# A hand-written order for the last two pairs of a two-layer graph kernel, and the norms at the change of passes in two parts

## The chip, the cores and the metric

The kernel runs on one core of a Trainium2 chip. The metric is the device time of one execution in microseconds (us), as the median of three runs. The engines are named as the profile names them: PE is TensorE (PEld its weight loads), DVE is VectorE, ACT is ScalarE, POOL is GpSimd, SP is the engine that only issues DMAs here. Each engine runs its own list of instructions strictly in order and waits on semaphores.

## The reference

Two graph layers on `x` of 128 graphs x 64 nodes x 768 features, with an adjacency of ones and zeros. Both are of the form `x + layer(relu(layernorm(x)))`.

```python
# layer 0: three products of 768 x 768 after neighbour averages, plus a table of relations
ctx = matmul(adj, hs @ Wadj.T + badj) / deg + matmul(radj, hs @ Wrev.T + brev) / rdeg + hs @ Wself.T + bself
rel = einsum('bij,bijr->bir', adj, E[rels]) @ Wr.T + br * deg + ...      # and the same for the reverse
# layer 1: attention with 6 heads of 128, and a gate
h = einsum('bni,hio->bhno', feat_in, W);  th = tanh(h)
attn = leaky(th @ w_src + (th @ w_dst).T);  attn = softmax(where(adj == 0, -999, attn))
feat_out = elu(concat(attn @ h + b))
gate = sigmoid(feat_in @ H_w.T + H_b)
out = gate * feat_out + (1 - gate) * feat_in
```

The result of layer 1 is added to its input `x`.

## The kernel before

The 8192 rows (graphs x nodes) are cut into 64 tiles of 128 rows (two graphs each), and these into 32 pairs. The kernel makes two passes over the pairs, one for each layer. Everything is float32.

**Products.** In both passes the products of a pair with the 768 x 768 weights go through a fast scheme for a 2 x 3 by 3 x 3 block product: 15 block products instead of 18. `A_SUMS` are the 11 sums f1 to f11 of the activations' blocks (`a00` to `a12`: first digit the tile of the pair, second the third of the features), `B_SUMS` those of the weights' blocks, `PRODUCTS` the 15 products, each with its PSUM bank (a, b, c or d), the output block it adds to and the sign. In pass 2 a product computes the heads' block (columns of `W`) and the gate's block (columns of `H_w`) side by side: `half_product` (L742) issues one matmul of 512 columns, 256 for the heads and 256 for the gate, and two of them make a product. `read` (L763) and `read_act` (L759) add the bank to the result in `hzs`: most reads are one DVE instruction of 512 columns over both halves; where a block gets its first value, ACT copies the heads' half and DVE adds the bias to the gate's half (256 columns each). A bank can be written again only when it has been read.

**Pass 1** is left to a scheduler. Its `finish` (L582) normalizes a pair's result for layer 1. For each tile k: `stats` (L229) takes mean and deviation on DVE (L233, L237, L239), the power -1/2 on POOL (L240) and the scaled mean on DVE (L241); ACT makes `hf` = relu of the norm (L588), which SP stores; POOL adds it to x (L590), SP stores that to the output; ACT makes `hh`, half of hf plus a half (L593), which SP stores. `hf` and `hh` share two buffers, so each waits until the one two before it has been stored.

**Pass 2** has its engines' order written out by hand: `ORDER` lists the steps of one pair, each with a lag (`R8/1` is the read of product 8 of the pair before), and the loop at its end walks this list for every pair; only SP is ordered by the scheduler. Steps: `Ta00` transposes a block on PE, `Ca00` copies it to SBUF on ACT (L732), `Ff1` forms a sum on DVE (L256, L258), `P1.0` is the first half of product 1, `R1` and `RA1` its reads on DVE and ACT. Then for each tile (0 or 1 of the pair): `th` tanh (L783), `mul` the products with w_src and w_dst (L787), `sum` their row sums on ACT (L797), `k` and `chain` the splitting of the sums in bf16 parts on POOL (L800 to L810), `rows`, `rrow`, `lrow`, `log` the logits (L822 to L839), `memset`, `cp`, `pre`, `tr`, `exp`, `rec` the masked softmax (L835 to L864), `turnp`, `pT` its transpose, `swap` a copy of heads between partitions by DMA (L816), `att` the attention (L888), `ev` the division, with bias, into f (L898, in two groups: even and odd heads), `g` the gate (L905), `e` the exponential (L909), `f0` to `f2` the end on DVE (L916, L918, L920), and `dma` the store (L923): POOL issues a DMA that adds f to the x which pass 1 stored in the output. A tile's f has two buffers.

Pair 31's `finish`, the last, runs within the first round of pass 2, in one piece at a quarter of the list, since pass 1 has no round after it. The bias `bb` of the heads (plus one) is loaded at the start of pass 2 (L682) and gets its one on DVE at L685.

Of the kernel before, what the change touches and what calls it, by code (L numbers as in the profile page):

```python
# [8 lines left out]
F32 = mybir.dt.float32  # L9
BF16 = mybir.dt.bfloat16  # L10
I32 = mybir.dt.int32
AF = mybir.ActivationFunctionType
OP = mybir.AluOpType
AX = mybir.AxisListType

P = 128
# [64 lines left out]
ORDER = """  # L81
# [6 lines left out]
turnp1/2 RA2 Ff11 e0/2 P1.1 P8.0 mul1/1 RA1 R1 P5.1 g1/1 pT1/2 rows0/1 R3 P4.0 lrow0/1 P6.0  # L88
f0.0/2 g0/1 att1/2 sum1.2/1 rec1/2 rrow0/1 f0.1/2 sum1.0/1 sum1.3/1 RA5 ev1.1/2 log0/1 swap1/1
sum1.1/1 swap0/1 P6.1 R5 ev1.0/2 e1/2 P4.1 P8.1 k1/1 R4 cp0/1 pre0/1 memset1/1 R6 P11.0 f1.0/2  # L90
""".split()


@with_exitstack
def kernel(
# [45 lines left out]
    nc = tc.nc  # L141
    G, N, D = x.shape
# [5 lines left out]
    H, DO = w_src.shape  # L148
# [32 lines left out]
    def row(v, parts):  # L181

        n = 1
        for s in v.shape:
            n *= s
        return bass.AP(tensor=v.tensor, offset=v.offset, ap=[[0, parts], [1, n]])
# [33 lines left out]
    dl = const.tile([P, H], F32, name="dl")  # L220
    nc.gpsimd.memset(dl, 0.0)

    def row_constants():
        for c in range(3):
            for i in range(NPART):
                a = c * HB + i * H
                nc.sync.dma_start(dl[a : a + H, :], ident[0:H, 0:H])

    def stats(src, to, behind=False):  # L229

        st = small.tile([P, 2, 6], F32, name="st")
        for i in range(2):
            ins = nc.vector.bn_stats(st[:, i, :], src[:, i * HALF : (i + 1) * HALF])  # L233
            if behind and i == 0:
                tc.keep_in_program_order(ins)
        mv = small.tile([P, 2], F32, name="mv")
        nc.vector.bn_aggr(mv, st.rearrange("p a b -> p (a b)"))  # L237
        ve = small.tile([P, 1], F32, name="ve")
        nc.vector.tensor_scalar(ve, mv[:, 1:2], EPS, None, op0=OP.add)  # L239
        nc.gpsimd.tensor_tensor(to[:, 0:1], ve, mhalf, op=OP.pow)  # L240
        nc.vector.scalar_tensor_tensor(to[:, 1:2], mv[:, 0:1], -1.0, to[:, 0:1],  # L241
                                       op0=OP.mult, op1=OP.mult)

# [59 lines left out]
    with ExitStack() as px:  # L305
# [273 lines left out]
                steps.append(lambda b=b, c=c: (counts(b, c, True), add(b, c)))  # L579
            return steps  # L580

        def finish(p):  # L582
            for k in range(2):
                t = 2 * p + k
                to = small.tile([P, 2], F32, name="rn")
                stats(X[t], to)
                h = keep.tile([P, D], F32, name="hf", bufs=2)
                nc.scalar.activation(h, X[t], AF.Relu, scale=to[:, 0:1], bias=to[:, 1:2])  # L588
                nc.sync.dma_start(H1D[p][k * P : (k + 1) * P, :], h)
                nc.gpsimd.tensor_add(X[t], X[t], h)  # L590
                nc.sync.dma_start(of[t * P : (t + 1) * P, :], X[t])
                hh = keep.tile([P, D], F32, name="hh", tag="hf", bufs=2)
                nc.scalar.activation(hh, h, AF.Identity, scale=0.5, bias=half)  # L593
                nc.sync.dma_start(HHD[p][k * P : (k + 1) * P, :], hh)

        def side(p):

# [46 lines left out]
                (24, lambda: count(0, 1)), (26, lambda: digits(0)),  # L644
                (68, lambda: count_t(0, 0)), (68, lambda: count_t(0, 1))]
        for p in range(NP):
            more = [(3, lambda: finish(p - 1))] if p else late
            if p == 1:
                more.append((10, row_constants))
            if p == NP - 1:  # L650
                more += fetch()
            merged(main(p), own(p) + side(p + 1) + more)


    with ExitStack() as px:
# [20 lines left out]

        load(0)
        hzs += [wb.tile([P, 2, D], F32, name=f"hz{i}") for i in range(4, NHZ)]

        bb = wb.tile([P, DO], F32, name="bb")  # L680
        wsd = wb.tile([P, 2, D], F32, name="wsd")
        nc.sync.dma_start(bb, row(b_att, P))  # L682
        nc.sync.dma_start(wsd[:, 0, :], row(w_src, P))
        nc.sync.dma_start(wsd[:, 1, :], row(w_dst, P))
        nc.vector.tensor_scalar(bb, bb, 1.0, None, op0=OP.add)  # L685
        mone = wb.tile([P, 1], F32, name="mone")
        nc.gpsimd.memset(mone, -1.0)
        de = wb.tile([P, H, N], BF16, name="de")
# [245 lines left out]
        def step(n, p):  # L934
            if n[0] in "TCF":
                {"T": turn, "C": copy, "F": form}[n[0]](p, n[1:])
            elif n[0] == "P":
                half_product(p, *(int(i) for i in n[1:].split(".")))
            elif n[0] == "R":
                (read_act if n[1] == "A" else read)(p, int(n.lstrip("RA")))  # L940
            elif "." in n:
                m, i = n.split(".")
                OF_TILE_PART[m[:-1]](2 * p + int(m[-1]), int(i))
            else:
                OF_TILE[n[:-1]](2 * p + int(n[-1]))

        order = [(n, int(k or 0)) for n, _, k in (x.partition("/") for x in ORDER)]
        px.enter_context(tc.manual_schedule(engines={
            mybir.EngineType.PE, mybir.EngineType.DVE, mybir.EngineType.Activation,
            mybir.EngineType.Pool}))  # L950
        for i in range(min(k for _, k in order), NP + max(k for _, k in order)):
            if i >= 0:
                load(i + 1)
            for j, (n, k) in enumerate(order):
                if i == 0 and j == len(order) // 4:
                    finish(NP - 1)
                if 0 <= i - k < NP:
                    step(n, i - k)


# [43 lines left out]
```

## Time and profile before

| | |
|---|---|
| median of 3 runs | 2537.05 us (2536.32 to 2537.84) |
| the profiled execution's own time | 2537.99 us |
| its span, first to last instruction | 2536.2 us |
| PE busy | 2460.0 us, 97% |
| DVE busy | 1983.1 us, 78% |
| ACT busy | 1073.5 us, 42% |
| POOL busy | 438.3 us, 17% |
| first transpose of pass 2 | at 1515.1 us |
| one round of pass 2 | 30.2 us (from the reciprocal of one pair, L864 at 2412.33, to the next at 2442.55) |
| last product of pass 2 starts | at 2491.07 us |

The page's busy times and slices are of one execution. A timeline's line gives the start in us from the span's start, the duration, the engine, the line of the kernel and the operation, what it writes and reads, and in brackets how long the engine stood idle before it and what ended that. In a window's row the numbers are the window, its length, and the busy time of PE, PEld, DVE, ACT and POOL with counts, then the granted clock of PE (1.00 is full), the DMA engines' share and GB/s. Consecutive DVE instructions overlap by about 0.085 us in the records, so an instruction of 0.42 us takes 0.335 us of the engine.

### The profile page before, as it was taken

How to read it: one execution, taken by the hardware profiler on the slowest of the kernel's cores; microseconds unless marked ns; L12 is line 12 of the kernel's file. 1: busy time of each engine (PE TensorE's matmuls, PEld its weight loads, DVE VectorE, ACT ScalarE, POOL GpSimd, SP SyncE). 2: the span in 40 equal slices, each digit the busy share in tenths (PEclk: the TensorE clock that was granted, in tenths of full speed). 3: DMA queues.
4: the chain of work that ended last, by engine and by line, in shares of the span. 5: the costliest groups of instructions: out<-in, count | busy, mean ns of one | idle time of the engine just before them, and what ended most of it. 6: DMA issues, size and time to landing. Idle time of an engine off the chain costs nothing.

```text
span 2536.2 us, 35252 instructions
## 1 busy us (share of the span) xinstructions
PE 2460.0 (97%) x12012; PEld 1713.6 (68%) x12012; DVE 1983.1 (78%) x4115; ACT 1073.5 (42%) x3586; POOL 438.3 (17%) x799
## 2 busy tenths in 40 slices
PE   5999999999999999999999998999999999999994
PEld 4788888888888888888888883444444444444442
DVE  8987777777777777777777555888888888888886
ACT  1222221222222212222222214777777777777775
POOL 0112121121221211212112111111111111111111
PEclk8999999999999999999999999999999999999996
DMA  5112122121121211211212143444444444444433
GB/s 174 58 53 104 52 82 74 52 104 53 59 98 53 91 66 53 104 53 69 88 53 99 52 150 118 102 104 106 102 107 110 102 108 110 109 114 103 96 75 75
DMA packets 114758, 224.17 MB, mean 88 GB/s; under 512 B 36506, under 2 KB 48397, under 8 KB 114578
## 3 DMA queue, kind: packets, MB, share of 16 engines
q1 hardware_dynamic: 105208, 196.70, 23.7%
q0 software_dynamic: 9216, 25.17, 6.4%
q8 instruction: 94, 1.54, 0.2%
q14 instruction: 86, 0.70, 0.1%
q10 hardware_dynamic: 154, 0.06, 0.0%
HBM read 95.67 MB, written 100.66 MB: 77 GB/s over the span
## 4 chain that ended last, share of the span: by engine, by line
PE 93%; DVE 2%; DMA 2%; issue 2%; POOL 1%; ACT 0%; SPq 0%; POOLq 0%; DVEq 0%; ACTq 0%
PE pwa L560 19%; PE pwb L560 16%; PE pma L745 13%; PE pmb L745 11%; PE pwc L560 7%; PE pwd L560 6%; PE pb L513 5%; PE pmc L745 5%; PE pmd L745 4%; PE ps L888 2%; PE ps L721 2%; PE pwd L544 1%; PE ps L870 1%; PE ps L839 1%; DVE weights L258 0%
## 5 line engine op out<-in xcount | busy, mean ns | idle before, releaser
L560 PE MATMUL pwa<-weights,op 128*128 128x256 f32 x2304 | 543.2, 383 | 4.5 <-DVE x L552 3.8
L560 PEld LDWEIGHTS pwa<-weights,op 128*128 128x128 f32 x2304 | 423.7, 190 | 73.6 <-DVE x L552 12.5
L521 ACT COPY op<-pb 128x768 f32<-128x768 f32 x160 | 124.2, 798 | 756.3 <-PE pb L513 756.3
L560 PE MATMUL pwb<-weights,op 128*128 128x256 f32 x1536 | 372.4, 383 | 11.4 <-DVE x L554 7.8
L258 DVE TENSOR_TENSOR op<-op 128x768 f32<-128x768 f32 x256 | 238.9, 953 | 156.0 <-ACT op L521 156.0
L560 PEld LDWEIGHTS pwb<-weights,op 128*128 128x128 f32 x1536 | 285.8, 191 | 59.1 <-DVE x L554 8.6
L745 PE MATMUL pma<-weights,op_f 128*128 128x512 f32 x640 | 318.0, 594 | 1.2 <-DVE weights L774 1.2
L797 ACT ACTIVATE pr<-pr 128x128 f32<-128x128 f32 x768 | 225.2, 295 | 24.2 <-DVE pr L787 24.2
L745 PE MATMUL pmb<-weights,op_f 128*128 128x512 f32 x384 | 197.4, 596 | 0.0
L745 PEld LDWEIGHTS pma<-weights,op_f 128*128 128x128 f32 x640 | 115.9, 191 | 120.3 <-issue 108.6
L240 POOL TENSOR_TENSOR rn<-ve,mhalf 128x1 f32<-128x1 f32 x128 | 106.9, 835 | 468.3 <-DVE ve L239 462.9
L560 PE MATMUL pwc<-weights,op 128*128 128x256 f32 x768 | 186.0, 385 | 0.0
L560 PE MATMUL pwd<-weights,op 128*128 128x256 f32 x768 | 176.2, 379 | 0.0
L513 PE MATMUL pb<-r,h 64*128 64x192 f32 x1536 | 152.7, 339 | 8.3 <-ACT h L422 8.0
L560 PEld LDWEIGHTS pwc<-weights,op 128*128 128x128 f32 x768 | 143.7, 191 | 25.1 <-issue 7.0
L492 POOL COPY c<-cnt 128x243 bf16<-128x243 bf16 x64 | 45.5, 740 | 659.2 <-PE pb L500 612.2
L560 PEld LDWEIGHTS pwd<-weights,op 128*128 128x128 f32 x768 | 145.9, 190 | 19.8
L233 DVE BATCH_NORM_STATS2 st<-x 128x6 f32<-128x384 f32 x256 | 134.5, 547 | 27.0 <-DMA x<-in_x_dram 25.2
L513 PEld LDWEIGHTS pb<-r,h 64*128 64x128 f32 x1536 | 124.1, 189 | 43.7 <-issue 30.5
L588 ACT ACTIVATE hf<-x,rn 128x768 f32<-128x768 f32 x64 | 65.8, 1028 | 194.4 <-issue 130.0
L745 PE MATMUL pmc<-weights,op_f 128*128 128x512 f32 x256 | 135.0, 609 | 10.3 <-DVE op_f L258 10.1
L797 ACT ACTIVATION_READ_ACCUMULATOR pr<-pr 128x1 f32 x768 | 144.1, 188 | 0.0
(174 smaller groups left out, 4228.2 us busy)
## 6 DMA issues: line engine op xcount, KB each, us to landing
x<-in_x_dram SPq DMA_DIRECT2D x64, 384.0 KB
h<-hf SPq DMA_DIRECT2D x64, 384.0 KB
out_dram<-x SPq DMA_DIRECT2D x64, 384.0 KB
hh<-hh SPq DMA_DIRECT2D x64, 384.0 KB
h<-h SPq DMA_DIRECT2D x64, 384.0 KB
x<-hh SPq DMA_DIRECT2D x64, 384.0 KB
out_dram<-f POOLq DMA_DIRECT2D x64, 384.0 KB, 6.1
hx<-weights SPq DMA_DIRECT2D x88, 192.0 KB
```

The costliest lines, as they stand in the source:

```text
L233: ins = nc.vector.bn_stats(st[:, i, :], src[:, i * HALF : (i + 1) * HALF])
L240: nc.gpsimd.tensor_tensor(to[:, 0:1], ve, mhalf, op=OP.pow)
L258: return (nc.vector.tensor_add if s1 == "+" else nc.vector.tensor_sub)(to, x, y)
L492: nc.gpsimd.tensor_copy(c3, CNT[p][:, k, :, None].to_broadcast([P, NROW, 3]))
L513: nc.tensor.matmul(ps[:, g, i * 3 * N : (i + 1) * 3 * N], H0[t][s, kb * P : (kb + 1) * P], rts[p % 2][s, k].rearrange("p s n -> p (s n)"), ...
L521: nc.scalar.copy(a.rearrange("p h s (g n) -> p g (h s) n", g=GT), ps[:, :, : 6 * N].rearrange("p g (x n) -> p g x n", n=N))
L560: nc.tensor.matmul(bank[b][:, :CQ], OPS[p, an][:, q, s, :], bw[bn][:, (s * KQ + q) * CQ : (s * KQ + q + 1) * CQ], start=(first and q == s ...
L588: nc.scalar.activation(h, X[t], AF.Relu, scale=to[:, 0:1], bias=to[:, 1:2])
L721: nc.tensor.transpose(ps[:, i, :], H1[2 * p + k][:, kb * P : (kb + 1) * P], ident)
L745: nc.tensor.matmul(bank[p, b], OPS[p, an][:, q, :], bw2[bn][:, 2 * q * CQ : 2 * (q + 1) * CQ], start=(first and q == 0), stop=(q == KQ - 1 ...
L797: nc.scalar.activation(PR[t][:, j, h, :], PR[t][:, j, h, :], AF.Copy, accum_out=to)
L888: nc.tensor.matmul(po[r][o, c, :], PT[t][s, c, o], (hs if r == g else HX[t])[s, 2 * c + r, :], start=True, stop=True)
```

## The change

The last rounds of pass 2 no longer follow `ORDER`. The loop ends with the round in which pair 29 is begun; a second list, `END`, holds all that is left: the whole of pairs 30 (lag 1) and 31 (no lag) and the rest of 29, 28 and 27. In it pair 31's products are not of 512 columns: `PH0` to `PH14` are the heads' products (two matmuls of 256 columns), `PG0` to `PG14` the gate's, each with a bank and a read of its own (`RH`, `RAH`, `RG`; six of the heads' reads on ACT, 24 reads of 256 columns on DVE). The heads' products come first, the gate's among the attention of the tiles before.

The ends of tiles 62 and 63 are done in two parts, even and odd heads (384 columns each): exponential, the three steps of the end, and the store. Tile 62 is still added into the output by POOL's DMA, in two parts. For tile 63 the x of the output is loaded (`xo`, on SP), added on DVE as a fourth step, and stored by SP.

At the change of passes `finish` is cut: for each tile one part with the statistics up to POOL's power and one with the scaled mean, the activations and the stores. The four parts of pair 31 are put after the 20th, 40th, 60th and 80th step of the first round. `bb` is loaded in pass 1, with the other constants of `row_constants`, and its one is added there.

```diff
+END = """
+tr0/3 f0.2/4 R8/2 Ta11/1 P7.0/2 Ta10/1 Ta00/1 Ca11/1 P9.0/2 Ca10/1 f1.1/4 Ca00/1 Ta02/1 P7.1/2
...
+P10.1/1 Ca01 f1.0/3 pT0/2 mul0/1 R10/1 PH2 sum0.3/1 log1/2 dma0/3 Ff10 P12.1/1 PH0 P13.0/1
+R12/1 RAH2 sum0.0/1 P14.0/1 P13.1/1 att0/2 f1.1/3 sum0.2/1 cp1/2 pre1/2 f1.2/3 P14.1/1 tr1/2
+sum0.1/1 R13/1 RAH0 ev0.0/2 PH3 PH1 exp1.0/2 PH5 R14/1 memset0/1 k0/1 ev0.1/2 chain0/1 rows0/1
+RH3 Ff11 RA14/1 th1/1 e0/2 PH8 RAH1 exp1.1/2 mul1/1 PH4 rrow0/1 PH6 f0.0/2 swap0/1 lrow0/1
+rec1/2 turnp1/2 sum1.1/1 sum1.0/1 sum1.3/1 RH4 pT1/2 memset1/1 log0/1 dma1/3 PH7 RH6 f0.1/2
+cp0/1 RAH5 PH9 f0.2/2 PH11 RAH7 pre0/1 att1/2 RH9 g1/1 tr0/1 RH8 k1/1 PG0 RH11 sum1.2/1 ev1.0/2
+PG5 g0/1 PH10 ev1.1/2 th0 chain1/1 PH12 RG0 mul0 RH10 rows1/1 rrow1/1 exp0.0/1 dma0/2 e1/2 PH13
+exp0.1/1 sum0.1 f1.0/2 RH12 PG3 PG2 lrow1/1 log1/1 sum0.0 RH13 swap1/1 f1.1/2 sum0.2 PH14
+rec0/1 PG1 RG2 sum0.3 cp1/1 turnp0/1 RG3 RAH14 pre1/1 f1.2/2 th1 RG1 tr1/1 PG6 k0 pT0/1 chain0
+mul1 exp1.0/1 exp1.1/1 PG4 dma1/2 rows0 rrow0 RG4 att0/1 PG8 lrow0 ev0.0/1 turnp1/1 memset0
+ev0.1/1 sum1.0 log0 PG7 memset1 pT1/1 RG6 rec1/1 e0/1 att1/1 sum1.2 RG5 PG9 cp0 sum1.1 sum1.3
+pre0 f0.0/1 PG11 RG7 f0.1/1 k1 ev1.0/1 ev1.1/1 tr0 RG9 e1/1 chain1 exp0.0 rows1 f0.2/1 RG11
+lrow1 rrow1 log1 swap1 exp0.1 f1.0/1 PG10 RG8 cp1 pre1 f1.1/1 tr1 turnp0 swap0 rec0 pT0 exp1.0
+f1.2/1 att0 exp1.1 RG10 PG12 dma0/1 ev0.0 ev0.1 e0.0 rec1 RG12 f0.0.0 PG13 RG13 f0.1.0 e0.1
+turnp1 PG14 g0 f0.0.1 RG14 f0.1.1 dma1/1 pT1 f0.2.0 att1 ev1.1 ev1.0 out0.0 f0.2.1 e1.1 f1.0.1
+e1.0 g1 f1.0.0 f1.1.1 f1.1.0 f1.2.1 f1.2.0 out0.1 f1.3.1 f1.3.0 out1.1 out1.0
 """.split()
...
+    bb = const.tile([P, DO], F32, name="bb")
+
     def row_constants():
+        nc.sync.dma_start(bb, row(b_att, P))
+        nc.vector.tensor_scalar(bb, bb, 1.0, None, op0=OP.add)
         for c in range(3):
...
-    def stats(src, to, behind=False):
+    def deviation(src, to, mv, behind=False):
...
         nc.gpsimd.tensor_tensor(to[:, 0:1], ve, mhalf, op=OP.pow)
+
+    def scaled_mean(to, mv):
+
         nc.vector.scalar_tensor_tensor(to[:, 1:2], mv[:, 0:1], -1.0, to[:, 0:1],
                                        op0=OP.mult, op1=OP.mult)
...
-        def finish(p):
-            for k in range(2):
-                t = 2 * p + k
-                to = small.tile([P, 2], F32, name="rn")
-                stats(X[t], to)
+        def finish(p, k):
+
+            t = 2 * p + k
+            to = small.tile([P, 2], F32, name="rn")
+
+            def norm_and_store():
+                scaled_mean(to, mv)
                 h = keep.tile([P, D], F32, name="hf", bufs=2)
...
+            mv = small.tile([P, 2], F32, name="mv")
+            return (lambda: deviation(X[t], to, mv), norm_and_store)
...
-            more = [(3, lambda: finish(p - 1))] if p else late
+            more = [(3, lambda: [f() for k in range(2) for f in finish(p - 1, k)])] if p else late
...
+        def whole_product(k, s):
+
+            p = NP - 1
+            an, bn, b, first = PRODUCTS[k][:4]
+            if first:
+                bank[p, b, s] = psm.tile([P, 512], F32, name=f"pm{b}", bufs=2 if b == "a" else 1)
+            for q in range(KQ):
+                nc.tensor.matmul(bank[p, b, s][:, :CQ], OPS[p, an][:, q, :],
+                                 bw2[bn][:, (2 * q + s) * CQ : (2 * q + s + 1) * CQ],
+                                 start=(first and q == 0), stop=(q == KQ - 1), skip_group_check=True)
...
+        def load_out(t):
+            if t in SUMMED_HERE:
+                XO[t] = keep.tile([P, D], F32, name="xo", tag="x", bufs=6)
+                nc.sync.dma_start(XO[t], of[t * P : (t + 1) * P, :])
...
+        def final_part(t, i, r):
+            f = part(FF[t], r)
+            if i == 0:
+                nc.vector.scalar_tensor_tensor(f, part(EE[t], r), 1.0, f, op0=OP.min, op1=OP.max)
+            elif i == 1:
+                nc.vector.scalar_tensor_tensor(f, f, 0.5, part(HM[t], r), op0=OP.mult, op1=OP.subtract)
+            elif i == 2:
+                nc.vector.scalar_tensor_tensor(f, part(hz(t)[1], r), 1.0, f, op0=OP.add, op1=OP.mult)
+            else:
+                nc.vector.tensor_add(f, f, part(XO[t], r))
+
+        def store_part(t, r):
+            to = part(of[t * P : (t + 1) * P, :], r)
+            if t in SUMMED_HERE:
+                nc.sync.dma_start(to, part(FF[t], r))
+            else:
+                nc.gpsimd.dma_start(to, part(FF[t], r), accum_op=OP.add)
...
-        for i in range(min(k for _, k in order), NP + max(k for _, k in order)):
+        ends = [f for k in range(2) for f in finish(NP - 1, k)]
+        order = parsed(ORDER)
+        SUMMED_HERE = (NT - 1,)
+        for i in range(min(k for _, k in order), NP - 2):
             if i >= 0:
                 load(i + 1)
             for j, (n, k) in enumerate(order):
-                if i == 0 and j == len(order) // 4:
-                    finish(NP - 1)
+                if i == 0 and j % 20 == 19 and ends:
+                    ends.pop(0)()
                 if 0 <= i - k < NP:
                     step(n, i - k)
+        load(NP - 1)
+        for n, k in parsed(END):
+            if k == 0:
+                last_step(n)
+            elif k < NP:
+                step(n, NP - 1 - k)
```

## The prediction

> **What bounds the kernel now.** I read the strip of 40 slices first, to find where TensorE (PE) is not full.
>
> ```profile
> PE   5999999999999999999999998999999999999994
> DVE  8987777777777777777777555888888888888886
> PEclk8999999999999999999999999999999999999996
> ```
>
> PE is full but for the start, the slice in which pass 2 begins, and the last. So only the change of passes and the end have time to give; between them PE sets the pace. VectorE (DVE), eight tenths busy in pass 2, comes next. The waits, for PE:
>
> ```profile
> PE pmc L745 <- DVE op_f L258: 10.1, 1, 10.1
> ```
>
> One hole of 10.1 us in front of the first product that reads f3. The order of time on DVE and ScalarE (ACT) shows what f3 waits for:
>
> ```profile
> 1516.84 0.53 DVE L258 TENSOR_TENSOR op_f<-op_a,op_a 128x256 f32<-128x256 f32 x1 [0.99 <-ACT op_a L732]
> 1520.41 0.23 DVE L685 TENSOR_SCALAR bb<-bb 128x128 f32<-128x128 f32 x1 [2.12 <-DMA bb<-in_b_att_dram]
> 1525.37 0.16 DVE L241 SCALAR_TENSOR_TENSOR rn<-mv,rn 128x1 f32<-128x1 f32 x1 [2.17 <-POOL rn L240]
> 1529.83 0.43 DVE L256 SCALAR_TENSOR_TENSOR op_f<-op_a,op_a 128x256 f32<-128x256 f32 x1 [3.63 <-ACT op_a L732]
> 1528.60 0.93 ACT L593 ACTIVATE hh<-hf,half 128x768 f32<-128x768 f32 x1 [1.96 <-DMA hh<-hh]
> ```
>
> Between f1 (first line) and f5 (fourth) DVE stands behind the load of bb and twice behind GpSimd's (POOL) power; then it waits for the copy of a02, which ACT does only after both tiles' hf and hh, the last of these held by a DMA (fifth line). Now the windows of the end (PE, PEld, DVE, ACT, POOL busy, then clock):
>
> ```profile
> 2480.00:2490.00 10.00, 8.76 (x25) 3.80 (x24) 9.76 (x16) 6.00 (x26) 2.14 (x3) 1.00 0.46 85
> 2490.00:2500.00 10.00, 6.06 (x58) 3.03 (x56) 7.40 (x16) 9.95 (x47) 1.24 (x6) 0.87 0.36 76
> 2500.00:2510.00 10.00, 2.00 (x9) 0.92 (x13) 7.29 (x14) 6.71 (x32) 4.90 (x9) 0.50 0.29 79
> 2510.00:2520.00 10.00, 4.15 (x51) 2.78 (x50) 5.12 (x15) 3.26 (x14) 0.74 (x1) 0.50 0.50 79
> 2520.00:2530.00 10.00, 0.00 (x0) 0.00 (x0) 3.77 (x5) 0.93 (x1) 1.75 (x2) 0.50 0.39 53
> ```
>
> The last product ends near 2492; 44 us of attention, ends and stores follow in which no engine is full. Two lines hold its largest waits:
>
> ```profile
> 2513.74 1.64 DVE L898 SCALAR_TENSOR_TENSOR f<-ps,dn,bb 128x128 f32<-128x128 f32 x6 [3.81 <-DMA out_dram<-f]
> 2525.10 1.75 POOL L923 DMA_DIRECT2D out_dram<-f  x2 [14.36 <-DVE f L920]
> ```
>
> The first waits for a store to free its buffer f; the second issues the last two stores, 11.1 us before the span's end at 2536.2.
>
> **What the Trainium skill says.** "TensorE: Matmul & The Clock Gate", What's actually happening: after an idle window of about 3.4 us the array runs at half rate until about 3.4 us of work. The trace agrees: after the hole, four passes of 512 columns starting at 1530.64 take until 1534.21, 3.57 us instead of 4 x 0.43 = 1.72, and the drain shows 0.50. "SBUF — State Buffer", SBUF: two separate sides: VectorE and GpSimd share a port pair as an exclusive lock. Here sdb's subtraction (L810) takes 0.22 us normally and 1.03 at 2502.74, beside a 768-wide DVE step; I use it for the range. "DMA: Bandwidth & Descriptors", Anatomy of one DMA: a GpSimd DMA costs about 2.0 us plus bytes/436 GB/s, 2.9 us for 384 KB; the trace's median for the accumulating store is 6.1 us, so I use the trace.
>
> **The change, part by part.** The build's order of instructions shows PE the same up to the last two pairs.
>
> *Change of passes.* bb's load and its +1 go to pass 1, where the load is issued beside dl's (SP, 29 us) and the DVE step stands behind the tv steps (61 us): the load has 30 us, the step costs about 0.14 us of DVE and pushes the dl and x loads behind it on SP by some 0.46 us; none gates PE there. Tile 62's statistics now stand ahead of pass 1's last additions and its power ahead of POOL's constants. New DVE order: f1, rn62, f8, f2, f5, f3, f7, statistics of 63, f9, a read, f4, a read, f6, rn63. ACT: five copies, hf62, hh62, the a02 copy, a read, hf63, hh63. Walk, with durations of these rows: f1 ends 1517.3; rn62 to 1517.45; hf62 (1.03) and hh62 (0.94) to 1519.5; a02's copy to 1519.85; f5 and f3 (starts 0.34 apart, 0.42 long) to 1520.6. PE is free at 1520.4: wait 0.25. Then f7, the statistics (1.01 + 0.2 + 0.15 and their hand-overs, 1.8), f9, a read and f4 end at 1523.4, while PE is free at 1521.5: wait 1.95. After it: hf63 waits for x+h of 62 (1.8 on POOL), the power and rn63 at 1524.2; hh63 ends 1526.3, the read behind it 1526.6; the product needing that bank comes four half products (3.4 us) after 1523.4, at 1526.9: no wait, but only 0.3 us of cover. Sum: holes of 2.2 instead of 10.06, **-7.8**. The clock is open: 1.25 us at 2489 left it full, 2.24 at 2497 halved it. I take a loss equal to before's (about 2 us in both), so up to 2 more could be gained; a late hh63 could cost 1.
>
> *The last two pairs.* DVE's order differs from 2419.75 on. From there it has 171 instructions in 105.1 us: 83.1 of work (durations less the 0.085 by which starts overlap), 21.3 in waits over 0.1 us, 0.7 in small ones. Added work: pair 31's reads were 6 of 256 columns (0.335 each) and 9 of 512 (0.60), 7.4 us; they become 24 of 256, 8.0: +0.6. The ends in halves (384 wide, 0.465 by the 384-wide row of 0.55): tile 62 six instead of three of 0.865, +0.2; tile 63 eight, since the residual is now added on DVE, +1.1. Together 85.1.
>
> Waits: I walked the five engines' lists in the new order, each instruction starting when its engine and what it reads are free, with the trace's durations. The same walk of the old list gives 21.2 us of waits and 104.7 in all where the trace has 21.3 and 105.1, so I trust it here. The new list leaves 6.6: 2.0 and 1.3 behind pair 30's reads on ACT, 1.2 for the last attention but one, the rest below 0.3. The old order had only tile chains left after the products. The new one finishes pair 31's heads first, so that tanh, sums and logits of tiles 62 and 63 start while the gate's products (12.9 us of PE) and their 15 reads still run and fill the gaps of these chains. DVE: 85.1 + 6.6 + 0.4 = 92.1 instead of 105.1, **-13.0**. DVE then carries the end; bounds of the waits are 3 (none but the three named halved) and 10 (the POOL lock twice, a late pT).
>
> PE: 120 passes of 256 columns for 60 of 512; in pass 1 twelve take 2.59 (0.216 each), so 25.9 us for 25.8: nothing. Holes of 2 us before the last tile's logits halve its clock there, which the walk holds. ACT: exps in halves, 2 x 0.52 for 0.93; only the last is on the path, and it lets DVE begin earlier.
>
> *Last stores.* Before: DVE ends 2524.85, the end is 11.35 later: two accumulating stores in one queue, landing 4.9 and 7.1 after their issue, then POOL's closing drain and the hand-shake, 3.4. Now tile 63 leaves by SP as plain halves of 192 KB, and tile 62's second half goes 3.7 before DVE's end. SP: issue 0.4, landing 3 (the hh store was ready 3.3 after issue), hand-shake 1.5: 4.5 to 5 after DVE. POOL: -3.7 + 5.9 + 3.4 = 5.6, or 6.8 if the drain's 9.8 us after issue is fixed. I take 6.2: **-5.1**. Unknown: 384 pieces of 512 bytes in place of 128 rows; cost from 1 us less (half the bytes) to 3 more (three times the 0.86 issue, twice). xo's load stands on SP some 25 us ahead of the new order and waits there for a buffer of tag x; behind it is only the last pair's adjacency, read more than 50 us later, and it has 100 us to land.
>
> Sum: 2536.2 - 7.8 - 13.0 - 5.1 = 2510.3 of span. The profiled execution took 2537.99, 0.94 over the median; the difference applied to the median 2537.05 gives **2511**.
>
> **Rivals.** (a) The end gains but the change of passes doesn't: the hole moves to the bank behind hh63. For it: 0.3 us of cover, and a wait there of 2 or 3 us would halve the clock. Against: hh63's DMA condition is met 2 us earlier. Price +6 to 7.8: 2518. (b) The end's waits stay near the old ones, because POOL's chain and small stores are slow: waits 12 instead of 6.6 and 3 us of stores: 2520. For it: the 1.03 us lock. Against: the old walk fits. (c) Slower: PE's clock falls to half at a hole early in the new order and stays, because the chain now lies between the products. PE has 60 us of work there and the walk leaves it some 30 us of room (92.1 less 62); -25.9 is eaten when more than about 56 us of work run at half rate. All of it: +32 over the room, 2536.2 + 6 = 2543 of time. Against: after the 10 us hole the clock came back within 3.6 us, and the walk shows no hole over 0.8 us until the last 20 us. (d) The edit does less than it says: the instruction lists show that it does move, so only a size can be off.
>
> **How the numbers follow.** Forecast 81%, (a) 9%, (b) 6%, no measurable change 2%, (c) 2%. About 0.2%, 5 us, is what a measurement of this kernel can tell from no change. Low end: -2 (clock), -2 (waits), -1 (stores): 2506; high: +1, +3.4, +3 by bounds, and (a): 2519. Faster 0.96, same 0.02, slower 0.02.
>
> **What would show it.** In the changed profile: the 10.1 us wait of pmc gone, two holes under 2.5 us near 1520; bb's step near 61 us; DVE over nine tenths full through the last slice but one, no wait for out_dram<-f; products until about 8 us before DVE ends; 5 to 7 us from DVE's end to the span's. Wrong if PE shows holes over 3 us in the last two pairs, the clock at 0.5 before the last 20 us, or stores landing over 9 us after DVE.

## The result, and the profile after

The changed kernel takes 2510.11 us (median of 4 runs, 2508.17 to 2512.95) where the kernel before, run beside it, takes 2536.69: a ratio of 0.9896 with a 95% interval of 0.9879 to 0.9913. The profiled execution took 2512.95 us, its span is 2511.2, so it is 2.8 us over its median; the one of before was 0.9 over its own.

To see where the 25.0 us of span went I cut both spans at three events: the first transpose of pass 2 on PE (the first `ps<-ident,h`), the start of the last new bank of pair 0 (product 8, the first `pmd<-weights,op_f` of pass 2), and the end of the last DVE instruction.

| stretch of the span, us | before | after | difference | predicted |
|---|---|---|---|---|
| pass 1, up to the first transpose | 1515.11 | 1514.33 | -0.8 | 0 |
| change of passes, first transpose to product 8 | 21.97 | 16.16 | -5.8 | -7.8 |
| product 8 to DVE's end | 987.73 | 976.79 | -10.9 | -13.0 |
| DVE's end to the end of the span | 11.40 | 3.89 | -7.5 | -5.1 |
| sum | 2536.2 | 2511.2 | -25.0 | -25.9 |

The strip of 40 slices of the changed kernel: PE's gap at the change of passes no longer shows in it, PE's last slice is at seven tenths instead of four, and DVE stays at eight tenths through the last slice.

```profile
PE   5999999999999999999999999999999999999997
DVE  8987777677777776786777655888888888888888
PEclk8999999999999999999999999999999999999998
```

The waits of PE in the changed kernel (line, what it waited for, us in total, times, longest). Those of pmc and pma stand where the 10.1 us stood, those of ps lie in the last 24 us:

```profile
PE ps L886 <- DVE rrow L873: 2.3, 1, 2.3
PE pma L792 <- DVE weights L819: 1.9, 1, 1.9
PE ps L869 <- POOL sdb L855: 1.9, 1, 1.9
PE pmc L792 <- DVE op_f L304: 1.4, 1, 1.4
```

The order of time at the change of passes, after (start, duration, engine, line, operation; in brackets the idle time before), first of all engines, then of PE alone:

```profile
1518.69 1.81 POOL L638 TENSOR_TENSOR x<-x,hf 128x768 f32<-128x768 f32 x1
...
1518.95 1.83 DVE L302 SCALAR_TENSOR_TENSOR op_f<-op_a,op_a 128x256 f32<-128x256 f32 x1 [1.70 <-ACT op_a L779]
...
1520.70 0.41 DVE L304 TENSOR_TENSOR op_f<-op_f,op_a 128x256 f32<-128x256 f32 x1
```

```profile
1521.17 1.12 PE L792 MATMUL pmc<-weights,op_f 128*128 128x512 f32 x2 [1.40 <-DVE op_f L304]
1524.19 2.08 PE L792 MATMUL pma<-weights,op_f 128*128 128x512 f32 x2 [1.90 <-DVE weights L819]
1526.06 1.92 PE L792 MATMUL pmb<-weights,op_f 128*128 128x512 f32 x2
1527.77 1.91 PE L792 MATMUL pma<-weights,op_f 128*128 128x512 f32 x2
1529.48 1.17 PE L792 MATMUL pmb<-weights,op_f 128*128 128x512 f32 x2
1530.49 1.02 PE L792 MATMUL pmd<-weights,op_f 128*128 128x512 f32 x2
```

Two things are to be seen. f5 (L302) took 1.83 us where the same step took 0.43 before; it ran beside POOL's addition of hf to x (L638), and f3 behind it (L304) was late by as much. And behind the second hole PE ran at half rate: pairs of passes take 1.9 to 2.1 us instead of 1.02, until 1529.8.

The windows of the end, after (window, length, busy PE, PEld, DVE, ACT, POOL, clock, DMA share, GB/s):

```profile
2480.00:2490.00 10.00, 5.59 (x46) 3.86 (x45) 9.71 (x27) 8.99 (x43) 2.16 (x8) 0.95 0.68 157
2490.00:2500.00 10.00, 9.43 (x47) 7.06 (x46) 8.01 (x20) 5.76 (x20) 1.35 (x2) 0.54 0.58 80
2500.00:2510.00 10.00, 0.93 (x25) 0.64 (x24) 7.12 (x18) 1.96 (x3) 2.33 (x2) 0.80 0.53 79
```

Before, 44 us with no engine full followed the last product; here the last product ends near 2500, 11 us before the span's end. DVE is at 9.7 of 10 to 2490 and at 8.0 in the next window, in which the clock stands at 0.54. The last stores and the last DVE instruction:

```profile
2501.81 1.18 POOL L1053 DMA_DIRECT2D out_dram<-f  x1 [6.94 <-DVE f L1044]
...
2503.83 1.15 POOL L1053 DMA_DIRECT2D out_dram<-f  x1 [0.83 <-DVE f L1044]
...
2506.26 1.02 DVE L1046 TENSOR_TENSOR f<-f,xo 128x384 f32<-128x384 f32 x2
2506.84 1.31 SPq L1051 DMA_DIRECT2D out_dram<-f  x2
```

### The profile page after: what moved, and what is told of

The parts are those of the page before. It is cut to its first block, busy times and chain, and to the rows that moved or that the text cites. A ratio compares the mean times of both kernels' runs of the same rounds, so it can differ in the third digit from the quotient of the medians.

```text
span 2511.2 us, 35383 instructions
## 1 busy us (share of the span) xinstructions
PE 2460.0 (98%) x12072; PEld 1724.7 (69%) x12072; DVE 1984.4 (79%) x4132; ACT 1073.6 (43%) x3588; POOL 440.4 (18%) x799
## 5 line engine op out<-in xcount | busy, mean ns | idle before, releaser
L304 DVE TENSOR_TENSOR op<-op 128x768 f32<-128x768 f32 x256 | 238.4, 951 | 154.7 <-ACT op L567 154.6
L792 PE MATMUL pma<-weights,op_f 128*128 128x512 f32 x620 | 309.5, 596 | 1.9 <-DVE weights L819 1.9
L844 ACT ACTIVATE pr<-pr 128x128 f32<-128x128 f32 x768 | 225.3, 295 | 25.2 <-DVE pr L834 25.1
L792 PE MATMUL pmb<-weights,op_f 128*128 128x512 f32 x372 | 192.2, 598 | 0.0
L606 PEld LDWEIGHTS pwc<-weights,op 128*128 128x128 f32 x768 | 143.2, 190 | 25.1 <-issue 7.0
L638 POOL TENSOR_TENSOR x<-x,hf 128x768 f32<-128x768 f32 x64 | 116.1, 1815 | 92.3 <-ACT hf L636 92.3
```

What stands on the lines that cost most here:

```text
L304: return (nc.vector.tensor_add if s1 == "+" else nc.vector.tensor_sub)(to, x, y)
L606: nc.tensor.matmul(bank[b][:, :CQ], OPS[p, an][:, q, s, :], bw[bn][:, (s * KQ + q) * CQ : (s * KQ + q + 1) * CQ], start=(first and q == s ...
L792: nc.tensor.matmul(bank[p, b], OPS[p, an][:, q, :], bw2[bn][:, 2 * q * CQ : 2 * (q + 1) * CQ], start=(first and q == 0), stop=(q == KQ - 1 ...
L844: nc.scalar.activation(PR[t][:, j, h, :], PR[t][:, j, h, :], AF.Copy, accum_out=to)
```

## The experiments

Each run is compared with runs of the kernel before on the same chip, so ratios may be compared throughout, times best within e1 to e4, e5 to e8, and e9 to e11, which share a chip each. The table has the median, the ratio to before with its interval, and the stretches of the profiled execution, cut as above ("last" is product 8 to DVE's end, "tail" DVE's end to the end of the span). Pass 1 is left out of the comparisons: its end lay anywhere from 1513.3 to 1515.7 us in these profiles, though PE's order in it is the same.

| run | median, us | ratio to before | change | last | tail |
|---|---|---|---|---|---|
| before | 2536.7 | 1 | 21.97 | 987.73 | 11.40 |
| after | 2510.1 | 0.9896 (0.9879 to 0.9913) | 16.16 | 976.79 | 3.89 |
| e1 pass change only | 2531.0 | 0.9978 (0.9970 to 0.9986) | 15.07 | 987.61 | 11.25 |
| e2 END only | 2516.3 | 0.9923 (0.9908 to 0.9937) | 21.10 | 975.22 | 3.78 |
| e3 one addition left out | 2509.8 | 0.9895 (0.9881 to 0.9910) | 13.70 | 976.90 | 3.80 |
| e4 norms one round later | 2508.5 | 0.9892 (0.9875 to 0.9908) | 9.91 | 977.09 | 3.81 |
| e5 gate with heads | 2519.1 | 0.9934 (0.9917 to 0.9950) | 15.09 | 982.77 | 3.98 |
| e6 POOL stores both | 2514.4 | 0.9918 (0.9903 to 0.9932) | 14.99 | 974.21 | 8.93 |
| e7 norms behind the sums | 2506.4 | 0.9886 (0.9871 to 0.9901) | 9.91 | 977.02 | 3.79 |
| e8 after, again | 2510.6 | 0.9902 (0.9887 to 0.9917) | 15.10 | 976.44 | 3.93 |
| e9 bb back in pass 2 | 2511.8 | 0.9907 (0.9892 to 0.9921) | 14.93 | 975.11 | 3.88 |
| e10 norms in one piece | 2515.6 | 0.9921 (0.9906 to 0.9936) | 20.80 | 975.20 | 3.80 |
| e11 e7 and two products moved | 2504.6 | 0.9877 (0.9860 to 0.9893) | 9.94 | 975.32 | 3.81 |
| e12 SP stores both | 2514.4 | 0.9911 (0.9894 to 0.9927) | 16.34 | 978.07 | 3.49 |

### Each part alone (e1, e2)

e1 keeps the change of passes and walks `ORDER` to the end; e2 keeps END and puts the norms and bb back.

```diff
# e1
-        for i in range(min(k for _, k in order), NP - 2):
+        for i in range(min(k for _, k in order), NP + max(k for _, k in order)):
...
-        load(NP - 1)
-        for n, k in parsed(END):
...
# e2 (and bb's load and one at the start of pass 2)
-                if i == 0 and j % 20 == 19 and ends:
-                    ends.pop(0)()
+                if i == 0 and j == len(order) // 4:
+                    for f in ends:
+                        f()
```

> The change of passes alone: norms of pair 31 in four parts and bb loaded in pass 1, with the old ORDER to the very end (no END). Theory (the parts add up, and the traces give each part's size): the first product 8 starts 5.8 us earlier, counted from pass 2's first transpose, and nothing else moves: 2530 to 2531 us, with the holes of 1.4 and 1.9 us before f3's and f4's products and f5 (SCALAR_TENSOR_TENSOR, 128x256) at 1.8 us. Rival 1 (the prediction's size was right and the changed kernel lost 2 us elsewhere): 2529 or less. Rival 2 (PE's head start at the change of passes is eaten by a later wait): 2535 to 2537.

> END alone: the last two pairs as in the changed kernel, but pair 31's finish in one piece at a quarter of the list and bb loaded at the start of pass 2, as before. Theory (parts add): 10.9 us from the waits of DVE and 7.4 us from the last stores, 18.3 together: 2518 to 2519 us, hole of about 10 us before f3's product. Rival (the end is worth what it was predicted, 18.1, or gives part of it back when the passes change later): 2521 or more.

The parts add. e1 is 5.2 us faster than the 2536.17 beside it, e2 19.9, together 25.1; both at once gave 26.6 and, in e8, 24.6. e1 came within its range; e2 is 1.7 us under its own, mostly because its last stretch lost 12.5 us and not the 10.9 of the changed kernel's profile. e1 moved only the change of passes, e2 only the other two stretches, but for 0.9 us: bb's load landed earlier in e2's execution (DVE waited 0.65 us for it instead of 2.12). e1 shows the same two holes, but a shorter half rate than the changed kernel's profile; these are its lines in order of time:

```profile
1524.18 2.07 PE L792 MATMUL pma<-weights,op_f 128*128 128x512 f32 x2 [1.90 <-DVE weights L819]
1526.05 1.79 PE L792 MATMUL pmb<-weights,op_f 128*128 128x512 f32 x2
1527.68 1.02 PE L792 MATMUL pma<-weights,op_f 128*128 128x512 f32 x2
1528.54 1.02 PE L792 MATMUL pmb<-weights,op_f 128*128 128x512 f32 x2
1529.39 1.02 PE L792 MATMUL pmd<-weights,op_f 128*128 128x512 f32 x2
```

From the second hole's end to product 8 this is 5.21 us, the changed kernel's profile has 6.30 for the same eight passes; at full rate they would take 3.44 (8 x 0.43).

### The shared port (e3)

```diff
-                nc.gpsimd.tensor_add(X[t], X[t], h)
+                if t != NT - 2:
+                    nc.gpsimd.tensor_add(X[t], X[t], h)
```

> The changed kernel with one POOL instruction left out: the 768-wide addition of hf to x for tile 62 at the change of passes (so that tile's part of the output lacks hf). Theory (the lock of the port that DVE and POOL share made f5 take 1.83 instead of 0.42 us): f5 takes 0.42 us, the hole before f3's product falls from 1.40 to about 0.25 us, the one before f4's stays between 1.5 and 2 us; 1 to 4 us faster, 2506 to 2509, depending on whether the clock still falls to half behind the second hole. Rival (f5 is long for another reason, for instance since it reads a02 just as ACT has written it): f5 still takes 1.8 us, time 2510.

f5 is back to 0.43 us, and PE no longer waits for f3: the line of f3's product has no bracket. The order of time in e3, of DVE and of PE:

```profile
1518.35 0.43 DVE L302 SCALAR_TENSOR_TENSOR op_f<-op_a,op_a 128x256 f32<-128x256 f32 x1 [1.70 <-ACT op_a L780]
1518.69 0.42 DVE L304 TENSOR_TENSOR op_f<-op_f,op_a 128x256 f32<-128x256 f32 x1
```

```profile
1519.17 1.12 PE L793 MATMUL pmc<-weights,op_f 128*128 128x512 f32 x2
1522.19 1.12 PE L793 MATMUL pma<-weights,op_f 128*128 128x512 f32 x2 [1.90 <-DVE weights L820]
1523.16 1.55 PE L793 MATMUL pmb<-weights,op_f 128*128 128x512 f32 x2
1524.50 1.92 PE L793 MATMUL pma<-weights,op_f 128*128 128x512 f32 x2
```

The change of passes is 13.70 us against 15.10 in e8: the hole of 1.40, exactly. That f5 was long by POOL's addition is thus shown. The time moved less (2509.8 against 2510.1 and 2510.6) and missed its range of 2506 to 2509; in the profile the last part, at 976.90, is one of the longer ones. The second hole remains, and behind it the rate halves, one pair of passes later than in e1.

### Where the norms stand (e4, e7)

e4 puts the four parts one round later; e7 puts both tiles' statistics behind the last f sum of round 0, tile 62's rest behind the reads that follow, tile 63's in round 1.

```diff
# e4
-                if i == 0 and j % 20 == 19 and ends:
+                if i == 1 and j % 20 == 19 and ends:
# e7
-        ends = [f for k in range(2) for f in finish(NP - 1, k)]
+        ends = [f for part in zip(*(finish(NP - 1, k) for k in range(2))) for f in part]
...
-                if i == 0 and j % 20 == 19 and ends:
+                for _ in range([(0, 93), (0, 93), (0, 117), (1, 39)].count((i, j))):
                     ends.pop(0)()
```

> The changed kernel with the four parts of pair 31's finish one round later (round 1 of pass 2 instead of round 0, same places in the list). Theory (the first round has no slack because its f sums start from nothing, while a later round has a fifth of DVE free): a02's copy follows the other five copies on ACT, f5 ends near 1517.3, both holes at the change of passes go (1.40 + 1.90) and with them the half clock (2.9 us): about 6 us faster than the changed kernel, 2504 us, and no PE hole over 0.5 us in round 1. Rival (the norms cost the same wherever they stand, since PE has no slack in any round): holes of 2 to 4 us turn up in round 1, 2507 to 2510.

> The changed kernel with pair 31's norms placed by where the engines are free: both tiles' statistics after the last f sum of round 0 (step 93), tile 62's scaled mean, activations and stores after RA5 and R5's neighbours (step 117), tile 63's at step 39 of round 1. Theory (the norms cost PE nothing where DVE, ACT and POOL are idle): the change of passes takes 9.9 us from the first transpose to product 8, as with the norms one round later (16.2 in the changed kernel), and the middle stays at 882.6 us (884.6 with the norms one round later, where sdb on POOL was 1.0 us late and a read on ACT 0.5): about 6 us less span than the changed kernel's profile, 2504 to 2506 us. Rival (they cost 2 us anywhere): 2506 to 2508.

In both, the change of passes falls to 9.91 us: no hole, no half rate, 5.2 us less than in e8 and 6.3 less than in the changed kernel's first profile. In e4 2.0 us of it come back in round 1: the part from product 8 to the first DVE instruction at which END's order differs from the old one takes 884.61 us, in before and after 882.63. One of e4's waits of PE, a sum of two:

```profile
PE ps L869 <- POOL sdb L855: 2.9, 2, 1.9
```

The sdb wait is one time and 1.0 us more than in the changed kernel: POOL's chain for the logits came behind tile 63's addition. So the theory of e4 was right at the change of passes and its rival for the round after, and the time, 2508.5, is the rival's. e7, placed by where the engines are idle, keeps 882.61 in that part: 2506.4 against 2510.6 of e8 on the same chip. That is 0.4 above its theory's range and within the rival's, but both numbers that the theory gave for the trace came, and the last stretch of this profile is a long one (977.02); its rival, 2 us lost wherever the norms stand, is refuted by the 882.61 beside the 9.91.

### Heads first (e5)

```diff
# the words of END
-PH2 ... RAH2 ... RH3 ... PG0 ... RG0
+P2.0 P2.1 ... RA2 R2 ... R3 ...
```

> The changed kernel, but pair 31's gate products are not put behind the heads': each product of END is one of 512 columns again (heads and gate side by side, at the place of PH), its read one of 512 columns at the place of RH, and PG and RG are gone. All else stays: halves at the end, stores, change of passes. Theory (heads first is what shortened the waits of DVE: 12.9 us of gate products and their reads now lie in front of the last tiles' tanh instead of beside their chain): DVE's idle time from the first changed instruction goes from 8.5 to 10 us back to 16 to 22, time 2516 to 2522. Rival (the order of the chains and the halves did it, DVE carries the end in either order): 2509 to 2512.

8.5 us slower than e8, and 6.3 of it between product 8 and DVE's end; DVE's idle time in its last part is 16.1 us, at the low end of the 16 to 22 expected. The theory held: that the heads' products come first is about half of what END takes from that stretch (-11 with it, -5 without). e5 also joins heads and gate in one instruction again, so the order and the split that makes it possible are tested together.

### The last stores (e6, e12)

```diff
# e6 (and no f1.3 in END)
-        SUMMED_HERE = (NT - 1,)
+        SUMMED_HERE = ()
# e12 (and f0.3.0, f0.3.1 in END)
+        SUMMED_HERE = (NT - 2, NT - 1)
```

> The changed kernel with tile 63 stored like tile 62: POOL's accumulating DMAs in halves, no load of xo and no fourth step on DVE. Theory (SP's plain store is what shortened the tail: POOL's stores land 5 to 7 us after their issue and its closing drain follows): DVE ends about 0.9 us earlier, but its end is then 9.5 to 11 us ahead of the span's instead of 3.9: 5 to 6 us slower than the changed kernel, 2515 to 2516. Rival (the halves shortened it, whoever issues them): about 0.5 to 1 us faster, 2509.

> The changed kernel with tile 62 ended like tile 63: its x loaded on SP, added on DVE in a fourth step for each half (two more DVE instructions of 384 columns, about 0.94 us), both halves stored by SP; POOL's last accumulating store is then tile 61's. Theory A (SP's last plain store sets the end of the changed kernel, 3.7 us from its issue to the span's end): the tail stays 3.8 to 4.0 us after DVE's end and the time rises by about 0.9, 2511 to 2512. Theory B (POOL's second half of tile 62 sets it, 7.4 us after its issue: 3.9 to landing and 3.5 of closing): the tail falls to 3.4 us or less and the time stays within 0.5 us, 2510 to 2511.

e6: the tail is 8.93 us instead of 3.93, and the time 3.7 over e8; the direction and mechanism as expected, the size 1.3 under the 5 to 6. Its tail is two halves issued one behind the other; the last landed 5.0 us after its issue (the median of the four halves is 3.9), and 3.5 more passed to the end of the span. e12: the tail fell by 0.4 to 3.49, nearly what theory B said, but its reason isn't shown. In the changed kernel's trace POOL's closing drain ends at 2510.39 and SP's at 2510.32, so the two paths are level to 0.07 us, and by the two traces most of the 0.4 is SP's own path, which was shorter in e12. The time rose, as theory A said, but by more than the 0.94 of DVE's two instructions, and the intervals of the ratios of e12 and e8 overlap. Its profile shows the last stretch longer by 1.3 to 1.6 and pass 1 by 0.7 to 1.7 than after and e8; the rest of its 3.8 us over e8 I can't place.

### The executions' spread (e8), bb and the split (e9, e10)

e8 is the changed kernel unchanged. e9 loads bb at the start of pass 2 again, e10 gives the norms in one piece (the last diff of e2).

```diff
# e9
-    bb = const.tile([P, DO], F32, name="bb")
...
+        bb = wb.tile([P, DO], F32, name="bb")
+        nc.sync.dma_start(bb, row(b_att, P))
...
+        nc.vector.tensor_scalar(bb, bb, 1.0, None, op0=OP.add)
```

> The changed kernel once more, to be compared with others of this call and to see how much one execution differs from the next. If PE's half clock after a hole of about 2 us lasts now about 3.5 and now about 7 us at random, the change of passes takes 15 or 16 us and DVE's last part 92.5 or 94.2 us, and the times spread over 2508 to 2513; if it is the same each time, both parts agree with the first profile to 0.1 us.

> The changed kernel with bb loaded and given its one at the start of pass 2 again (the norms stay in four parts). Theory (DVE stands behind bb's load, which landed 3.8 to 5.3 us after pass 2's first transpose in the profiles of before and of END alone; with tile 62's scaled mean behind it on DVE, hf, hh and the copy of a02 are late by as much): the hole before f3's product goes from 1.4 to between 3 and 5 us, 2512 to 2514 us. Rival (the load is hidden, since the copy of a02 ends the wait anyway): 2510 to 2511, hole 1.4.

> The changed kernel with pair 31's norms in one piece at a quarter of the list again (bb stays in pass 1). Theory (the split of the norms is worth far more than bb): only bb's wait of 0.7 to 2.1 us goes, the change of passes takes 19 to 20.5 us from the first transpose to product 8 (21.1 with both undone, 15.1 to 16.2 with both), 2514 to 2516 us. Rival (bb was what held it): 17 us or less, 2512 or less.

e8 has the same holes (1.4, 1.9, 1.9, 2.3) to 0.1 us, but 15.10 at the change of passes where the first profile has 16.16. So the holes are the program's, and what the clock does behind them differs from one execution to the next. e9: the rival held at the change of passes, though the time is 0.8 over its range. bb's step waited 1.02 us on DVE, but behind tile 62's scaled mean and in front of f5, which had 0.43 us more to wait for the copy of a02; the hole before f3's product is 1.37, and the 1.2 us of time over e8 is not in the stretches. e10: the theory held in the time and, to 0.3 us, at the change of passes; bb alone in pass 1 brings 0.3 us over e2's profile (20.80 against 21.10) and 1.2 over that of before, in which DVE waited 1.5 us longer for the load. The split of the norms is nearly the whole gain at the change of passes.

### A version faster than both (e11)

e7 with two of the gate's products moved in END, to fill PE's holes before the last tile's rows and logits:

```diff
-... rows1 f0.2/1 RG11 lrow1 rrow1 log1 ... PG10 ... RG10 PG12
+... PG10 rows1 f0.2/1 RG11 lrow1 RG10 rrow1 PG12 log1 ...
```

> The norms placed as in the run that put them behind the f sums, and in END two of the gate's products of pair 31 moved up: PG10 ahead of the last tile's rows and PG12 ahead of its logits (with the read of PG10), to fill PE's holes of 1.9 and 2.3 us there. Theory (the holes cost little by themselves, but they halve PE's clock, and DVE then waits 1 to 2.5 us for the last attention and gate products): PE stays at full clock to 2496, DVE's idle time in the last part falls from 8.5 to 10.2 us to 7 to 8.5, 1 to 2 us faster than without: 2504 to 2505.5. Rival (DVE carries the end, or the hole only moves to behind the logits, where the next product waits for its bank): 2506 to 2507.

2504.6 us (2504.12 to 2505.13): 5.5 to 6 us under the changed kernel, 31.3 under the one before, 1.8 under e7. The two holes fell to 1.0 and 0.9, but another came behind the last tile's logits, and the clock fell there, at 2485.4: the time that the theory gave came, without PE at full clock to 2496, which was its reason. The waits of e11:

```profile
PE ps L935 <- ACT pT L922: 1.9, 1, 1.9
...
PE ps L869 <- POOL sdb L855: 1.0, 1, 1.0
PE ps L886 <- DVE rrow L873: 0.9, 1, 0.9
```

Its last stretch is 975.32, that of e2, e9 and e10 without this edit 975.1 to 975.2: it isn't shorter than their best. e7's profile had 977.02. The clock was at half for 6.8 us in the one and 10.2 in the other. So the moved products may only make the long half rate rarer; with four runs each, and intervals of the ratios that overlap, how much of the 1.8 is theirs stays open.

## Why the prediction was right, point by point

The forecast was 2511 and 2510.1 came, but its three terms were off by 2.0 to 2.4 us each, and the sum holds since the errors have both signs. That the total came within 1 us is luck; what each part was to do came, the sizes less well.

**Change of passes, -7.8: too much by 2.0 in the profile, by 0.9 in e8.** The order, the second hole (1.95 predicted, 1.90) and product 8 without a wait came as walked. The step that failed is the first hole, "f5 and f3 (starts 0.34 apart, 0.42 long)": 0.25 us predicted, 1.40 measured. Everything that f5 waits for was in time; the walk had POOL's addition as a thing that others wait for, not as one that shuts DVE out. I had cited the exclusive lock of the Trainium skill, "SBUF — State Buffer", SBUF: two separate sides, and used it only for the range at the end. The section says for whom it holds: a DVE instruction with two inputs in SBUF against a POOL instruction that reads SBUF. f5 and the addition are such a pair, and e3 shows it with 1.83 against 0.43. e7 has the counterpart: a DVE instruction with one input in PSUM beside the same addition, and the next with two in SBUF (order of time):

```profile
1539.77 1.81 POOL L638 TENSOR_TENSOR x<-x,hf 128x768 f32<-128x768 f32 x1 [9.59 <-ACT hf L636]
...
1540.11 0.69 DVE L821 TENSOR_TENSOR weights<-weights,pmb 128x512 f32<-128x512 f32 x1 [1.87 <-PE pmb L792]
...
1540.72 1.15 DVE L304 TENSOR_TENSOR op_f<-op_a,op_a 128x256 f32<-128x256 f32 x1
```

The first, at 0.69, is as long as alone, the second ends 0.3 after POOL.

The other open term, the clock ("a loss equal to before's (about 2 us in both)"), came in two sizes: with the same two holes the change of passes takes 14.9 to 15.1 us in e1, e5, e6, e8 and e9 (a loss of 1.8 in e1) and 16.2 to 16.3 in the changed kernel's first profile and e12 (a loss of 2.9). The granted clock was at half for 3.4 us in the first group and 6.8 in the second; the last section has what goes with it.

**bb.** Its step costs nothing in pass 1, at 63.05 us where 61 was predicted. That was right; but it brings nothing either, once the norms are split (e9).

**The last two pairs, -13.0: measured -10.9, and -12.5 where the half rate was short.** Three terms were off. Work, by the prediction's own count, was 84.1 us instead of 85.1. Waits under 0.1 us were 1.4 instead of 0.4, which takes that back. Waits over 0.1 us were 8.6 instead of 6.6 in the first profile, 7.1 in e2: this is the term that was missed. The waits that it named came: 2.1 and 1.2 behind ACT's reads (2.0 and 1.3 predicted), 0.9 before the last attention but one (1.2). Those that it didn't have are 0.3, 0.8 and 0.2 behind gate products at half rate. The longest ends at 2498.62, when DVE's read of pmb (L1017) has waited 0.82 us for the product. The order of time of PE shows why, after:

```profile
2489.83 0.48 PE L886 MATMUL ps<-rrow,lrow 82*128 82x384 bf16 x1 [2.31 <-DVE rrow L873]
2490.10 1.91 PE L1002 MATMUL pmb<-weights,op_f 128*128 128x256 f32 x4
...
2494.80 2.07 PE L1002 MATMUL pma<-weights,op_f 128*128 128x256 f32 x4
2496.67 1.91 PE L1002 MATMUL pmb<-weights,op_a 128*128 128x256 f32 x4
...
2499.02 1.10 PE L1002 MATMUL pma<-weights,op_f 128*128 128x256 f32 x4
```

and in e2, where the rate is full again by the second product behind the same hole:

```profile
2494.56 0.48 PE L885 MATMUL ps<-rrow,lrow 82*128 82x384 bf16 x1 [2.32 <-DVE rrow L872]
2494.84 1.91 PE L1001 MATMUL pmb<-weights,op_f 128*128 128x256 f32 x4
...
2499.54 1.13 PE L1001 MATMUL pma<-weights,op_f 128*128 128x256 f32 x4
2500.51 1.03 PE L1001 MATMUL pmb<-weights,op_a 128*128 128x256 f32 x4
```

The prediction's text has a half rate behind these holes in its walk, but gives no length for it. The clock was at half for 10.2 us in the first profile, for 6.8 in e2. The reason it gave for the gain, heads first so that chains and products lie side by side, is shown by e5.

**Last stores, -5.1: measured -7.5.** The plan was right (tile 63 by SP, tile 62's second half well ahead of DVE's end). Mis-sized were both paths: POOL 5.6 to 6.8 predicted, 3.9 measured, since a half lands 3.9 us after its issue where I took 5.9 for it (the 3.4 from the landing to the end came as taken, 3.45); SP 4.5 to 5 predicted, about 3.8 in the changed kernel and 3.5 in e12, with a landing about 2.5 us after the second half's issue where 3 was taken, and 0.9 to 1.2 from there to the end instead of 1.5. The prediction read DVE's end before as 2524.85; it is 2524.81. The issue of a half costs POOL 1.17 us instead of 0.88, the dearer side of the bounds, but it is not on the path.

**The rivals.** (a), a wait at product 8 behind hh63, didn't come: product 8 follows at once. (b), long waits at the end, has a small part in it, 2 us. (c), slower by the clock: the half rate came in the last two pairs, but only from 2488.9 on, 22 us before the end, and for 10.2 us. (d) is refuted by e1 and e2, which each move the stretch that they should.

**The signs.** One sign of being wrong did come: the clock at 0.5 before the last 20 us, though by 2 us only; the longer wait behind it is the 1.6 us by which this profile's last stretch exceeds e2's. DVE was not over nine tenths full to the end (9.7 of 10 us to 2490, 8.0 in the next 10), and the tail of 3.9 us is under its 5 to 7.

## What to carry to other kernels

A step that is moved must be asked not only what it waits for, but what runs beside it on the engine that shares its port: 1.8 us of POOL cost DVE 1.4 us and PE a hole. Work that nobody waits for (the norms here) belongs where its engines are idle, found in the trace, and not spread evenly over a list: e7 gained 4.2 us by four positions. A hole of 2 us before a stretch of products is to be priced with the half rate behind it, which here cost about as much again (1.8 and 2.9 us), and to different amounts in two executions of one program.

## What the runs showed of the hardware

- The granted clock in the traces is either full or half, and in all 14 profiles every change of it within the span lies, in one execution, on a grid of 3.41 us. Where the grid lies differs from one execution to the next. So the half rate lasts whole steps. At the change of passes it is 3.41 us in e1, e3, e5, e6, e8 and e9, 6.83 in the changed kernel's first profile and e12, and 10.24 with the long hole in before, e2 and e10. Behind the holes at the end it is 6.83 in e2, e4, e6, e9, e10 and e11, and 10.24 in the first profile, e3, e7, e8 and e12; in before, e1 and e5, with longer holes there, it lasts to the end.
- It is PE's idle time within one step of the grid, and not the length of one hole, that goes with the fall. From 100 us on, steps at full rate with up to 1.75 us of idle time were followed by full rate, those with 1.83 us or more by half. In the first profile the step up to 1522.95 holds the hole of 1.40 and 0.66 us of the next one; in e3, without the first hole, the step up to 1523.52 holds the 1.90 alone, and the half rate begins 1.3 us after the hole's end. These times are read off the records, in which PE's ends are modelled; no run set the grid or the idle time.
- The Trainium skill, "TensorE: Matmul & The Clock Gate", What's actually happening, has a free-running window of about 3.4 us, and the grid agrees with it. Its condition for the fall, "after ≥1 idle window (~3.4µs)", doesn't: steps a little over half idle were followed by half rate.
- The lock seems to work both ways: in e4 a POOL multiplication of 128 x 12 (L847), 0.2 to 0.5 us in 63 of its 64 places, took 1.73 us in the one place where it stood beside a DVE multiplication of 1.78 us (L834) that started 0.12 us before it. No run took that DVE step away.
- Accumulating stores of half a tile, in pieces of 512 bytes, landed 3.9 us after their issue, whole tiles 4.8 (two of each, changed kernel, after 2480 us), and cost POOL 1.17 instead of 0.88 us to issue.
